# Causal attention on one Trainium2 core: the four diagonal squares of a block in one score tile, the rest of the diagonal unmasked

## The chip, the cores and the metric

The kernel runs on one core of a Trainium2 chip. The metric is device time in microseconds (us) of one execution: the median of the runs before is 1833.45 us.

The core has a matrix engine (TensorE, in the profile PE, with its weight loads as PEld), a vector engine (VectorE, DVE), a scalar engine (ScalarE, ACT), GpSimd (POOL) and an engine that issues DMAs (SyncE, SP). Each takes its own instructions in order; semaphores tie them together. TensorE writes its results into PSUM, which DVE and ACT read.

## What is computed

Two transformer layers on 2048 tokens of width 256. Each is a layer norm with causal attention (16 heads of 16), and a layer norm with an MLP (2048 wide, weights dequantised from packed codes). The first attention has rotary angles, biases and 4 key and value heads; the second has 16 and neither. What matters here is the attention:

```python
scores = jnp.einsum('bthd,bshd->bhts', q, k) * scale
causal = jnp.tril(jnp.ones((S, S), dtype=bool))
scores = jnp.where(causal[None, None, :, :], scores, -jnp.inf)
probs = jax.nn.softmax(scores, axis=-1)
attended = jnp.einsum('bhts,bshd->bthd', probs, v).reshape(B, S, hidden)
```

## The kernel before

**Units.** Queries go in 4 blocks `b` of 512 (4 tiles of 128), heads in 4 groups `g` of 4. A group is two pairs `p` of two heads `r`; the two heads of a pair lie in rows 0-63 and 64-127 of the matrix engine, so that two matmuls run side by side. A unit is one (b, g): 16 units per attention, 32 in all. Each unit has two passes over its keys.

**Maxima** (`max_steps`). For each block of keys `c` up to `b`, each query tile `i` and each pair, `scores` makes a score tile with queries on the partitions (L787), and DVE reduces it to a maximum per query and head (L799, tile `mx`). In the diagonal block, `c == b`, the tile is (i + 1) * 128 keys wide, and its last 128 columns, a square on the diagonal, are masked first. `gather` (L808) joins the maxima of the blocks and writes them as three bf16 parts into `m_pad`; `turn` (L826) transposes these on TensorE (L835), and ACT keeps them as `mT` (L841).

**Values** (`value_steps`). For each key tile `kt` and each pair, `pair` makes a score tile with keys on the partitions: first the "lift", which puts the negated maxima into PSUM (L884, weights `sel`), then the scores on top (L889). ACT takes the exponentials (L901) into `e`. On the diagonal, a tile begins at its own queries (`q0`), so that it is 512, 384, 256 or 128 columns wide, and its first 128 columns are masked. `values` multiplies `e` with the values and a column of ones, four heads in four column strips of the array (L869, f32, two instructions a matmul), into one accumulator `av`; it goes in halves of 256 queries. `end` copies `av` out, `divide` transposes it (L923) and divides.

**Masks.** `add_mask` (L756) adds very negative numbers to a 128x128 square by matmuls of a bf16 pair: two parts of 64 columns for each of two heads, so four matmuls of 64 columns (L762). They are not issued at once: the tile puts them, with what follows, into `self.owed`, and `settle` (L767) issues them at the next score tile of the kind, or at the next step of the value pass. Until then the tile stays in PSUM.

**PSUM.** A score tile is two banks, `[128, 2, 512]` f32, one per head. There are three of them, for both passes and the MLP (`ps_s`); `av` and a general tile `ps_m` have one bank each.

**Order.** It is written out by hand. `run` (L974) takes unit after unit: the value steps of this one are the main line, and beside them go the maxima of the next one, blended with preparations for the next block, output projections and dequantisation. `weave` (L43) spreads the side steps evenly over the main ones, with none beside the last three (`rest=3`). A main step is a tuple: its score tile, then the side steps, then its value matmuls. The first three steps of a unit have a share of their own (L1034 to L1036); the last unit's `end` and `divide` are put behind steps 0 and 2 of the next (L1025), and the next unit's `turn` ahead of the last step (L1028). The first unit's maxima run in the preparation of block 0, each followed by some idle matmuls (`fill`, L697). SP loads the queries of later units (`load_q`), GpSimd the keys (`load_k`).

Of the kernel before, what the change touches and what calls it, by code (L numbers as in the profile page):

```python
# [9 lines left out]
F32 = mybir.dt.float32  # L10
# [6 lines left out]
AF = mybir.ActivationFunctionType  # L17
# [4 lines left out]
P = 128  # L22
# [58 lines left out]
def tile_hybrid_layers(  # L81
# [329 lines left out]
    class Attention:  # L411
# [30 lines left out]
        def prep_steps(self, b, alone=False, load=False, picks=None, amid=(), fill=None):  # L442
# [245 lines left out]
            if picks:  # L688


                of = lambda f, c: lambda: f(c, krows if c == 2 else P)
                steps.append(lambda: fill(3))
                steps += [of(f, c) for c in (2, 0) for f in (pair, rotated_pair, high, low)]
                steps += [of(pair, 1), lambda: set_keys(2, krows), lambda: fill(2), set_queries]
                steps.append(lambda: fill(3))
                steps += [lambda: self.load_k(b, 2, 1), lambda: self.load_q(b, 1)]
                for step, idle in zip(amid, (0, 0, 1, 1, 2, 2, 2, 0, 1)):  # L697
                    steps += [step, lambda idle=idle: fill(idle)]
                steps[-1:-1] = [lambda: value(0), lambda: value(1)]
                self.after = [lambda: keep_value(0), lambda: keep_value(1)]  # L700
                self.after += [of(f, 1) for f in (rotated_pair, high, low)]
                self.after += [lambda: self.load_q(b, 2), add_bias]
                return steps
            else:
                kc = [*range(2, (D + krows + P - 1) // P)]
                for c in [*kc, 0, 1] if alone else [0, *kc, 1]:
                    n = min(P, D + krows - c * P)
                    if c == 1 and alone:
                        steps.append(values)
                    steps.append(holding(lambda c=c, n=n: plain(c, n)))  # L710
                    steps += [holding(lambda c=c, n=n: high(c, n)), lambda c=c, n=n: low(c, n)]
                    if c >= 2:
                        steps.append(lambda c=c: self.load_k(b, c))
                    elif c == 0 and load:
                        steps += [lambda g=g: self.load_q(b, g) for g in range(2)]
# [37 lines left out]
            return self.kT[c][64 * r : 64 * r + 64, g if self.first else 2 * g + p, at]  # L753

        @staticmethod
        def add_mask(pt, kind, at):  # L756

            for part in range(2):
                to = slice(at + 64 * part, at + 64 * part + 64)
                for r in range(2):  # L760
                    rows = slice(64 * r, 64 * r + 64)
                    nc.tensor.matmul(  # L762
                        pt[:, r, to], lhsT=mask_w[rows, kind, part, :],
                        rhs=mask_t[rows, kind, part, :], start=False, stop=(part == 1),
                    )

        def settle(self, kind=None):  # L767
# [8 lines left out]
        def max_steps(self, b, g):  # L776

            held = {}

            def scores(i, c, p):  # L780
                if not held:
                    held["mx"] = self.wk.tile([P, NT, 4, NB], F32, tag="mx", name="mx")
                w = TB if c < b else (i + 1) * P
                self.settle("max")
                pt = ps_s()
                for r in range(2):
                    nc.tensor.matmul(  # L787
                        pt[:, r, :w],
                        lhsT=self.qT[b, g][64 * r : 64 * r + 64, p, i * P : (i + 1) * P],
                        rhs=self.key_rows(c, g, p, r, slice(0, w)),  # L790
                        start=True, stop=(c < b),
                    )

                def masked():
                    self.add_mask(pt, 0, w - P)
                    reduced()

                def reduced():
                    nc.vector.tensor_reduce(  # L799
                        held["mx"][:, i, 2 * p : 2 * p + 2, c], pt[:, :, :w], AX.X, ALU.max  # L800
                    )

                if c == b:
                    self.owed.append(("max", masked))
                else:
                    reduced()

            def gather():  # L808
                self.settle()
                nm = self.wk.tile([P, NT, 4], F32, tag="nm", name="nm")  # L810
                nc.vector.tensor_reduce(
                    nm, held["mx"][:, :, :, : b + 1], AX.X, ALU.max, negate=True
                )

                to = m_pad[:, :, :, :6].rearrange("q t r (p s) -> q t p r s", s=3)
# [25 lines left out]
                nc.scalar.copy(self.mT[b, g], pt)  # L841


            tiles = [(i, c) for c in range(b + 1) for i in range(NT)]
            steps = [lambda i=i, c=c, p=p: scores(i, c, p) for i, c in tiles for p in range(2)]
            return steps + [gather], turn

        def value_steps(self, b, g):

            nk = NT * (b + 1)  # L850
            held = {"pending": []}

            def values(half):


                self.settle()
                kt, q0, es_ = held["pending"][0]
                whole = (b, g) == (NB - 1, NG - 1)
                few = whole or TB - q0 <= TB // 2
                if half == 1:  # L860
                    held["pending"].pop(0)
                if few and half != whole:
                    return
                if kt == 0 and half == whole:
                    held["av"] = ps_av()
                own = slice(q0, TB) if few else slice(*((q0, TB // 2), (TB // 2, TB))[half])
                for j in range(4):
                    h = g if self.first else 4 * g + j
                    nc.tensor.matmul(  # L869
                        held["av"][32 * j : 32 * j + 32, own],  # L870
                        lhsT=self.vv[kt // NT][:, kt % NT, h * VW : h * VW + 32],
                        rhs=es_[j // 2][:, j % 2, own],
                        start=(kt == 0 and half == whole), stop=(kt == nk - 1),
                    )

            def pair(kt, p):
                q0 = max(0, kt - NT * b) * P
                diagonal = kt >= NT * b
                keys = slice((kt % NT) * P, (kt % NT + 1) * P)
                self.settle()  # L880
                pt = ps_s()

                for r in range(2):
                    nc.tensor.matmul(  # L884
                        pt[:, r, q0:], lhsT=sel[64 * r : 64 * r + 64, p, :],
                        rhs=self.mT[b, g][64 * r : 64 * r + 64, q0:], start=True, stop=False,
                    )
                for r in range(2):
                    nc.tensor.matmul(  # L889
                        pt[:, r, q0:], lhsT=self.key_rows(kt // NT, g, p, r, keys),  # L890
                        rhs=self.qT[b, g][64 * r : 64 * r + 64, p, q0:],
                        start=False, stop=not diagonal,
                    )
                e = self.wk.tile([P, 2, TB], F32, tag="e", name="e", bufs=4)

                def masked():
                    self.add_mask(pt, 1, q0)
                    exponentials()

                def exponentials():  # L900
                    nc.scalar.activation(e[:, :, q0:], pt[:, :, q0:], AF.Exp, scale=QK_SCALE)  # L901

                if diagonal:
                    self.owed.append(("exp", masked))
                else:
                    exponentials()
                if p == 0:
                    held["es"] = [e]
                else:
                    held["pending"].append((kt, q0, held["es"] + [e]))  # L910

            def end():
                values(0)
                values(1)
                o = pre.tile([P, TB], F32, tag="o", name="o")
                nc.scalar.copy(o, held["av"])
                held["o"] = o
# [16 lines left out]
                )  # L934

            steps = []
            for kt in range(nk):
                for p in range(2):
                    scored = lambda kt=kt, p=p: pair(kt, p)
                    steps.append((scored, lambda p=p: values(p)) if kt else scored)  # L940
            return steps, end, divide

        def out_steps(self, b):
# [30 lines left out]
        def run(self, extra, beside):  # L974
# [17 lines left out]
            for n, (b, g) in enumerate(units):  # L992
# [30 lines left out]
                steps, end, divide = self.value_steps(b, g)  # L1023

                for at, step in zip((0, 2), ending):  # L1025
                    scored, *summed = steps[at] if isinstance(steps[at], tuple) else (steps[at],)
                    steps[at] = (scored, step, *summed)
                if turn:  # L1028
                    scored, summed = steps[-1]
# [1 line left out]
                if (b, g) == (0, 3):  # L1031

                    maxima = blend(maxima[:-1], [zeros] * 8) + maxima[-1:]
                first = len(maxima) * 3 // len(steps)  # L1034
                weave(steps[:3], lead + maxima[:first])
                weave(steps[3:], blend(maxima[first:], more) if maxima else more, rest=3)  # L1036
                ending = [end, divide]
            end()
            return [divide] + self.out_steps(NB - 1)
# [197 lines left out]
```

## Time and profile before

| | us |
|---|---|
| runs | 1833.45, 1830.45, 1834.42; median 1833.45 |
| span of the profiled execution | 1830.9 |
| median less that span | 2.55 |
| TensorE busy | 1748.1 |
| DVE busy | 1123.5 |
| ACT busy | 808.1 |
| first attention, first to last `mT` | 38.2 to 509.9 |
| second attention, first to last `mT` | 949.3 to 1454.0 |

The span is that of one profiled execution, and the profiler gives no other time for it; what the median has beyond the span lies around the first and last instruction. A busy TensorE is not TensorE at its peak, since matmuls are pipelined and a record's length has latency in it: distances between the starts of matmuls tell what they cost. A row of a group reads: line, engine, operation, output and inputs, count, busy time, mean ns of one, and the idle time of the engine before it with what ended it. Units of block 0 take 13 to 25 us from one `mT` to the next, those of block 3 some 46 to 52. The maxima of the first unit of an attention run ahead of it, so 32 units share one pattern; the last unit of each attention has no maxima beside it, but MLP work.

### The profile page before, as it was taken

To read this page: it belongs to the slowest core of one execution; us is meant where nothing else is said; L and a number is where in the kernel's file an instruction comes from. 1 tells how busy PE (TensorE), PEld (TensorE's weight loads), DVE (VectorE), ACT (ScalarE), POOL (GpSimd) and SP (SyncE) were. 2 spreads that over 40 slices of the span, in tenths; PEclk is the share of its full clock that TensorE was granted. 3 is DMA by queue.
4 is the path that set the end of the run, shared out by engine and by line. 5 is a ranking of instruction groups with operands and counts; after the bars stand their busy time and mean duration, and the time that the engine had idled before them with its cause. 6 is when DMAs were issued, how large, how long until landed. Compare 5 with 4: busy or idle time off the path is not lost.

```text
span 1830.9 us, 31568 instructions
## 1 busy us (share of the span) xinstructions
PE 1748.1 (95%) x13313; PEld 913.3 (50%) x13313; DVE 1123.5 (61%) x1679; ACT 808.1 (44%) x1080; POOL 239.8 (13%) x444
## 2 busy tenths in 40 slices
PE   8888899899999999999998999999999999999999
PEld 4444444444443474746464444444444445655646
DVE  5576887887884626262644767767877626354442
ACT  2435556566667313131314455655666753132221
POOL 4122202110013101012101000000000001111010
PEclk9899999999999999999999999999999999999999
DMA  5240400120002100005006132032000000000000
GB/s 139 68 93 32 94 24 30 48 50 24 19 13 76 52 1 0 1 0 125 2 1 117 24 76 53 22 60 59 13 13 2 11 37 1 12 3 9 7 6 12
DMA packets 43134, 65.40 MB, mean 36 GB/s; under 512 B 14000, under 2 KB 21040, under 8 KB 42736
## 3 DMA queue, kind: packets, MB, share of 16 engines
q1 hardware_dynamic: 34352, 47.37, 9.0%
q0 software_dynamic: 7680, 15.48, 4.9%
q8 instruction: 105, 1.72, 0.4%
q10 hardware_dynamic: 960, 0.52, 0.1%
q14 instruction: 37, 0.30, 0.1%
HBM read 43.45 MB, written 17.83 MB: 33 GB/s over the span
## 4 chain that ended last, share of the span: by engine, by line
PE 74%; DVE 15%; ACT 7%; issue 2%; DMA 1%; POOL 0%; ACTq 0%; DVEq 0%; SPq 0%; POOLq 0%
PE ps_s L1086 24%; DVE mx L799 12%; PE ps_av L869 10%; PE ps_s L884 7%; PE ps_s L787 6%; PE ps_m L1111 6%; PE ps_av L1111 6%; ACT e L901 5%; PE ps_s L889 5%; PE ps_m L504 2%; PE ps_m L963 2%; PE ps_s L762 1%; ACT mT L841 1%; PE ps_s L504 1%; PE ps_m L923 1%
## 5 line engine op out<-in xcount | busy, mean ns | idle before, releaser
L799 DVE TENSOR_REDUCE mx<-ps_s 128x2 f32<-128x1024 f32 (+3 forms) x640 | 660.3, 1061 | 216.7 <-PE ps_s L762 109.0
L901 ACT ACTIVATE e<-ps_s 128x1024 f32<-128x1024 f32 (+3 forms) x640 | 568.8, 898 | 374.1 <-PE ps_s L889 219.5
L869 PE MATMUL ps_av<-e,v 128*32 128x256 f32 (+2 forms) x4384 | 350.7, 391 | 0.0
L889 PE MATMUL ps_s<-qT,kT 64*128 64x512 f32 (+3 forms) x1280 | 333.8, 519 | 0.0
L787 PE MATMUL ps_s<-kT,qT 64*128 64x512 f32 (+3 forms) x1280 | 266.5, 418 | 34.2 <-DVE mx L799 15.3
L884 PE MATMUL ps_s<-mT,sel 64*128 64x512 bf16 (+3 forms) x1280 | 229.9, 353 | 26.1 <-ACT mT L841 11.0
L1086 PE MATMUL ps_s<-xnT,wg 128*128 128x512 f32 x512 | 240.9, 593 | 0.0
L1086 PE MATMUL ps_s<-xnT,wu 128*128 128x512 f32 x512 | 240.6, 592 | 0.0
L884 PEld LDWEIGHTS <-sel 64*128 64x128 bf16 x1280 | 75.5, 93 | 252.4 <-issue 241.8
L787 PEld LDWEIGHTS ps_s<-kT,qT 64*128 64x128 f32 x1280 | 127.6, 185 | 142.8 <-ACT e L901 67.3
L1092 ACT ACTIVATE t<-ps_s 128x512 f32<-128x512 f32 x128 | 76.3, 596 | 243.9 <-PE ps_s L1086 243.7
L1095 ACT ACTIVATE t<-t 128x512 f32<-128x512 f32 x128 | 80.6, 629 | 199.0 <-DVE t L1094 199.0
L1094 DVE TENSOR_TENSOR t<-ps_s,t 128x512 f32<-128x512 f32 x128 | 88.2, 689 | 123.3 <-POOL t L1093 121.1
L1086 PEld LDWEIGHTS ps_s<-xnT,wu 128*128 128x128 f32 x512 | 97.3, 190 | 122.5 <-issue 122.5
L1093 POOL TENSOR_SCALAR t<-t 128x512 f32<-128x512 f32 x128 | 79.0, 618 | 534.4 <-ACT t L1092 530.8
L1086 PEld LDWEIGHTS ps_s<-xnT,wg 128*128 128x128 f32 x512 | 95.1, 190 | 104.2 <-issue 102.5
L1096 DVE SCALAR_TENSOR_TENSOR t<-t,ps_s 128x512 f32<-128x512 f32 x128 | 88.0, 687 | 89.0 <-ACT t L1095 89.0
L869 PEld LDWEIGHTS ps_av<-e,v 128*32 128x32 f32 x4384 | 87.3, 108 | 93.2 <-issue 78.9
L889 PEld LDWEIGHTS ps_s<-qT,kT 64*128 64x128 f32 x1280 | 128.4, 195 | 0.0
L1111 PE MATMUL ps_m<-wd,inter 128*128 128x256 f32 x512 | 114.5, 380 | 0.0
L1111 PE MATMUL ps_av<-wd,inter 128*128 128x256 f32 x512 | 114.5, 380 | 0.0
L1111 PEld LDWEIGHTS ps_av<-wd,inter 128*128 128x128 f32 x512 | 96.7, 190 | 17.1 <-issue 4.5
(147 smaller groups left out, 1192.8 us busy)
## 6 DMA issues: line engine op xcount, KB each, us to landing
qT<-h SPq DMA_DIRECT2D x248, 64.0 KB, 2.2
kT<-h POOLq DMA_DIRECT2D x88, 128.0 KB, 5.8
h<-high SPq DMA_DIRECT2D x24, 256.0 KB, 2.1
h<-low SPq DMA_DIRECT2D x24, 256.0 KB, 3.1
wd<-wd_kept SPq DMA_DIRECT2D x2, 2048.0 KB, 8.2
wd_kept<-dq_d SPq DMA_DIRECT2D x4, 512.0 KB, 2.7
out<-x SPq DMA_DIRECT2D x16, 128.0 KB, 1.7
x<-x SPq DMA_DIRECT2D x3, 512.0 KB, 7.5
```

The lines of the kernel that those rows point to most:

```text
L787: nc.tensor.matmul(pt[:, r, :w], lhsT=self.qT[b, g][64 * r : 64 * r + 64, p, i * P : (i + 1) * P], rhs=self.key_rows(c, g, p, r, slice(0, w)),
L799: nc.vector.tensor_reduce(held["mx"][:, i, 2 * p : 2 * p + 2, c], pt[:, :, :w], AX.X, ALU.max)
L869: nc.tensor.matmul(held["av"][32 * j : 32 * j + 32, own], lhsT=self.vv[kt // NT][:, kt % NT, h * VW : h * VW + 32], rhs=es_[j // 2][:, j % ...
L884: nc.tensor.matmul(pt[:, r, q0:], lhsT=sel[64 * r : 64 * r + 64, p, :], rhs=self.mT[b, g][64 * r : 64 * r + 64, q0:], start=True, stop=False,)
L889: nc.tensor.matmul(pt[:, r, q0:], lhsT=self.key_rows(kt // NT, g, p, r, keys), rhs=self.qT[b, g][64 * r : 64 * r + 64, p, q0:], start=Fals ...
L901: nc.scalar.activation(e[:, :, q0:], pt[:, :, q0:], AF.Exp, scale=QK_SCALE)
L1086: nc.tensor.matmul(pt[:, k, :], lhsT=w[:, c, fc * P : (fc + 1) * P], rhs=self.xnT[b][:, c, :], start=(c == 0), stop=(c == 1),)
L1093: nc.gpsimd.tensor_scalar(t, t, GELU_A, 1.0, ALU.mult, ALU.add)
L1094: nc.vector.tensor_tensor(t, gate, t, ALU.mult)
L1095: nc.scalar.activation(t, t, AF.Tanh, scale=GELU_C)
L1096: nc.vector.scalar_tensor_tensor(t, t, 1.0, gate, ALU.add, ALU.mult)
L1111: nc.tensor.matmul(po[:, :D], lhsT=inter[:, fc, i * P : (i + 1) * P], rhs=wd[:, fc, :], start=(fc == 0), stop=(fc == NFC - 1),)
```

## The change

In the diagonal block both passes are cut otherwise. The four 128x128 squares on the diagonal, one per query tile, go side by side into one score tile per pair; one set of four mask matmuls, now 256 columns each (64 in each of the four squares), masks them all. What is left under the diagonal needs no mask:

- Maxima: query tile 3 has 384 keys per pair, in a tile as before. Query tiles 2 and 1 have 256 and 128 keys per pair; both pairs go side by side into one tile. The unmasked part's maxima have a column of their own in `mx` (`NB + 1` columns); query tile 0 has no such part, and GpSimd writes the very negative number there. Six tiles in place of eight, in the order 3, 3, squares, squares, 2, 1.
- Values: key tile 0 of the block has 384 queries per pair, key tiles 1 and 2 have 256 and 128, both pairs in one tile. Six tiles in place of eight, in the order 0, 0, squares, squares, 1, 2. The value matmuls are `rest(0)`, 384 wide, behind the first squares; `own`, 4 x 4 of 128 columns, behind key tile 1; `rest(1)` behind key tile 2; `rest(2)` in `end`.
- Score matmuls: 28 in place of 16 per unit and pass, with the same columns in all. Mask matmuls: 16 in place of 64 per unit. Value matmuls on the diagonal: 28 in place of 24.
- `run`: in block 0 one step, not three, has its own share. In the first preparation, seven maximum steps with five idle matmuls take the place of nine with nine.

```diff
-                for step, idle in zip(amid, (0, 0, 1, 1, 2, 2, 2, 0, 1)):
+                for step, idle in zip(amid, (0, 0, 1, 1, 2, 0, 1)):
...
+                    to = pt[:, r, :].rearrange("p (n c) -> p n c", c=P)
                     nc.tensor.matmul(
-                        pt[:, r, to], lhsT=mask_w[rows, kind, part, :],
-                        rhs=mask_t[rows, kind, part, :], start=False, stop=(part == 1),
+                        to[:, :, 64 * part : 64 * part + 64], lhsT=mask_w[rows, kind, part, :],
+                        rhs=mask_t[rows, kind, part, :].unsqueeze(1).broadcast_to([64, NT, 64]),
+                        start=False, stop=(part == 1),
                     )
...
+                    held["mx"] = self.wk.tile([P, NT, 4, NB + 1], F32, tag="mx", name="mx")
+                    nc.gpsimd.memset(held["mx"][:, 0, :, b + 1], NEG)
                 self.settle("max")
                 pt = ps_s()
...
+                if c < b:
+                    product(pt, 0, i, c, p, slice(0, TB))
+                    maximum(mx[:, i, heads, c], pt)
+                elif i == 0:
+                    for n in range(NT):
+                        at = n * P
+                        product(pt, at, n, b, p, slice(at, at + P), n == 0, False)
+
+                    def masked():
+                        self.add_mask(pt, 0)
+                        maximum(
+                            mx[:, :, heads, b], pt.rearrange("q r (n k) -> q n r k", k=P)
+                        )
+
                     self.owed.append(("max", masked))
+                elif i == NT - 1:
+                    product(pt, 0, i, b, p, slice(0, i * P))
+                    maximum(mx[:, i, heads, b + 1], pt[:, :, : i * P])
                 else:
+                    for n in range(2):
+                        product(pt, n * i * P, i, b, n, slice(0, i * P))
+                    maximum(
+                        mx[:, i, :, b + 1].rearrange("q (p r) -> q p r", r=2),
+                        pt[:, :, : 2 * i * P].rearrange("q r (p k) -> q p r k", p=2),
+                    )
...
+            tiles = [(i, c, p) for c in range(b) for i in range(NT) for p in range(2)]
+            tiles += [(i, b, p) for i in (NT - 1, 0) for p in range(2)]
+            tiles += [(i, b, 0) for i in (2, 1)]
...
+            def both_pairs(kt):
+                q0 = (kt + 1 - first) * P
+                queries, w = slice(q0, TB), TB - q0
+                self.settle()
+                pt = ps_s()
+                for p in range(2):
+                    lift(pt, p * w, p, queries, p == 0)
+                for p in range(2):
+                    score(pt, p * w, p, kt, queries, p == 1)
+                e = held["e"][kt] = new_e()
+                exponentials(e[:, :, : 2 * w], pt[:, :, : 2 * w])
+
+            def squares(p):
+                self.settle()
+                pt = ps_s()
+                lift(pt, 0, p, slice(0, TB))
+                for n in range(NT):
+                    score(pt, n * P, p, first + n, slice(n * P, (n + 1) * P), False)
+                e = held["e"]["own", p] = new_e()
+
+                def masked():
+                    self.add_mask(pt, 1)
+                    exponentials(e, pt)
+
+                self.owed.append(("exp", masked))
...
+            def own():
+                self.settle()
+                for n in range(NT):
+                    to = slice(n * P, (n + 1) * P)
+                    product(
+                        first + n, to, lambda j: held["e"]["own", j // 2][:, j % 2, to]
+                    )
...
             steps = []
-            for kt in range(nk):
+            for kt in range(first + 1):
                 for p in range(2):
...
+            steps += [
+                (lambda: squares(0), lambda: rest(0)), (lambda: squares(1),),
+                (lambda: both_pairs(first + 1), own),
+                (lambda: both_pairs(first + 2), lambda: rest(1)),
+            ]
...
+                some = 3 if b else 1
+                first = len(maxima) * some // len(steps)
+                weave(steps[:some], lead + maxima[:first])
+                weave(steps[some:], blend(maxima[first:], more) if maxima else more, rest=3)
```

`first` is the first key tile of the unit's own block, `product` in the value pass makes four matmuls, one per head.

## The prediction

> **What bounds the kernel now.** I first read the share of each engine, the chain that ended last and the costliest groups, all on the page:
>
> ```profile
> PE 1748.1 (95%) x13313; PEld 913.3 (50%) x13313; DVE 1123.5 (61%) x1679; ACT 808.1 (44%) x1080; POOL 239.8 (13%) x444
> ...
> PE 74%; DVE 15%; ACT 7%; issue 2%; DMA 1%; POOL 0%; ACTq 0%; DVEq 0%; SPq 0%; POOLq 0%
> ...
> L884 PE MATMUL ps_s<-mT,sel 64*128 64x512 bf16 (+3 forms) x1280 | 229.9, 353 | 26.1 <-ACT mT L841 11.0
> ```
>
> TensorE ends 74% of the span. What DVE adds (15%) comes in pairs of reductions during which TensorE waits for a score tile. The third line shows one wait for `mT` in each of the 32 units, 0.34 us (11.0 / 32). Then the groups by shape:
>
> ```profile
> L799 DVE TENSOR_REDUCE mx<-ps_s 128x2 f32<-128x1024 f32 x448 | 533.1, 1221 | 122.2 <-PE ps_s L787 99.2 <-PE ps_s L762 15.3
> ...
> L762 PE MATMUL ps_s<-mask_t,mask_w 64*128 64x64 bf16 x2048 | 100.9, 195 | 0.0
> ...
> L799 DVE TENSOR_REDUCE mx<-ps_s 128x2 f32<-128x256 f32 x64 | 26.6, 421 | 34.8 <-PE ps_s L762 34.0
> ...
> L835 PE MATMUL ps_m<-ident_b,m_pad 128*128 128x128 bf16 x128 | 12.7, 222 | 4.9 <-DVE m_pad L822 4.5
> ```
>
> 2048 mask matmuls are 64 per unit, in 16 groups of four. A reduction costs about 154 ns plus 1.042 ns an element: (1221 − 421) / 768 and the remainder. TensorE's durations contain pipeline latency, so its costs are taken as distance between starts. The end of a unit on TensorE, one row per group:
>
> ```profile
> 1357.87 0.28 PE L884 MATMUL ps_s<-mT,sel 64*128 64x256 bf16 x2
> 1357.91 0.36 PE L889 MATMUL ps_s<-qT,kT 64*128 64x256 f32 x2
> 1358.12 0.23 PE L762 MATMUL ps_s<-mask_t,mask_w 64*128 64x64 bf16 x4
> 1358.28 0.43 PE L869 MATMUL ps_av<-e,v 128*32 128x128 f32 x8
> 1358.64 0.28 PE L884 MATMUL ps_s<-mT,sel 64*128 64x256 bf16 x2
> ...
> 1359.04 0.64 PE L869 MATMUL ps_av<-e,v 128*32 128x256 f32 x8
> 1359.62 0.23 PE L884 MATMUL ps_s<-mT,sel 64*128 64x128 bf16 x2
> 1359.65 0.31 PE L889 MATMUL ps_s<-qT,kT 64*128 64x128 f32 x2
> 1359.80 0.23 PE L762 MATMUL ps_s<-mask_t,mask_w 64*128 64x64 bf16 x4
> ...
> 1361.61 0.39 PE L884 MATMUL ps_s<-mT,sel 64*128 64x512 bf16 x2 [0.32 <-ACT mT L841]
> ```
>
> Lift and scores of a tile take 0.25 us at 256 columns, 0.18 at 128 (elsewhere 0.35 at 384, 0.46 at 512). Eight value matmuls take 0.36 at 128 columns and 0.57 at 256, so 0.785 at 384. Until the last line nothing waits: the diagonal end of a unit is TensorE's. One more row gives the price of a fresh set of weights under a short matmul:
>
> ```profile
> 34.34 2.00 PE L640 MATMUL ps_av<-wqkv_a,xnT 128*128 128x64 f32 x16
> 36.17 0.38 PE L1146 MATMUL ps_m<-zeros 128*128 128x512 bf16 x1
> ```
>
> 16 matmuls, each with its own 128 columns of f32 weights, come 114 ns apart (1.83 / 16), although they move only 64 columns.
>
> **The change, part by part, per unit** (32 units). Columns stream at 0.417 ns (a 512-wide pair of score matmuls, rows 0-63 and 64-127 at once, follows the last after 213).
>
> 1. Masks. Four 64-wide ones take 67 ns when scores follow, of which 2 x 27 stream. 16 groups: 1,072. After: 4 groups of 2 x 107 + 13 = 227, together 908. **−0.16.** The columns stay the same, only the overhead goes. A matmul that writes four pieces of 64 with gaps is nowhere in the trace; bounds 908 and 4 x 4 x 67 = 1,072, and I take 908 since streaming is what both rows share. The Trainium skill, PSUM — Partial Sum Buffer, section Specifications (TRN2), speaks against it: an access pattern that is not contiguous "slows matmuls significantly". No row here tests it; at half rate, my estimate, the masks would cost 1.7 and the kernel 27 us more.
>
> 2. Squares. A 512-wide score pair becomes four 128-wide pairs, each with weights of its own; nothing stands between them, so the next pair's load lies under 53 ns of streaming only. I take 115 a pair, the row above: three pairs of four are 62 longer, four such tiles: **+0.74.** Bounds: 53 a pair (load hidden, +0) and 146 (the transposes at L923, four in 0.585 us, also a load each; +1.12). The Trainium skill, TensorE: Matmul & The Clock Gate, section Back-to-back issue gap, gives about 81 ns for a 128-column matmul in a stream of load and matmul; by it the squares would cost 0.34 and the sum would be 13 us lower. The 114 measured here is for f32 weights, and I keep it.
>
> 3. Both pairs in one tile. Maxima: second load under 107 or 53 of streaming, +0.01 and +0.06. Exponentials: 0.474 for two of 0.244, 0.366 for two of 0.186, −0.02. **+0.05.**
>
> 4. Values. Before: groups of 0.57, 0.57, 0.36, 0.57, 0.57, 0.36: 3.00. After: 0.785, eight sets of four at 133 plus 92 to leave (from the 0.36 and 0.57) = 1.156, 0.57, 0.36: 2.87. Two groups fewer; entering one costs 90 (score pair to value matmul 508, to score pair 418). **−0.31.**
>
> 5. Tiles. Two maximum tiles fewer; about half of them wait for a tile to come free and then show a load of some 105. **−0.11.** DVE and ACT have two instructions fewer each, 0.31 and 0.34 (ACT by 1027 and 386: about 172 an instruction). Off the path while TensorE ends the unit.
>
> TensorE: −0.16 + 0.74 + 0.05 − 0.31 − 0.11 = **+0.21**, times 32 = +6.8 us.
>
> 6. A new wait. The value matmuls of the squares (`own`) follow the first two-pair tile, and need the exponentials of the second square tile. Those start 0.12 after its mask and take 1.03, landing 0.05 later; TensorE has 0.47 of scores and 0.09 of entering to do: **+0.63**, times 32 = +20.2. Queued behind it on TensorE: the rest of `own`, `turn`, the last tile. No maxima are left to fill it: `weave` with rest=3 puts none beside the last three steps.
>
> 7. Waits that go. `rest(1)` (0.66 with entry) now stands between `turn` and the next unit, and hides `mT`: 30 x 0.34 = −10.2. `gather` is issued some 4 us before `turn` instead of 2.3, so the wait for `m_pad` goes: −4.5.
>
> 8. Tile turnover. In the diagonal phases TensorE waits 17.5 us for a reduction or exponential (added up from its idle rows: 10.8 in the units of block 0, 4.6, 1.9 and 0.2 in blocks 1 to 3). 12 tiles instead of 16 turn over, 4 instead of 16 are held for a mask. Bounds 0 and −17.5; I take half: −8.8.
>
> 9. Pace before the diagonal. Maxima go into two steps fewer: block 3 has 28 in 24 instead of 30 in 26, block 2 has 20 in 16 instead of 22 in 18, block 1 has 12 in 8 instead of 14 in 10. At 1.22 a reduction DVE needs 1.5 to 7% more per dense step, about 0.3 a unit, 21 units: 0 if TensorE paces them, +6.5 if DVE does; half: +3.2.
>
> 10. GpSimd gets a memset per unit for the extra column of `mx` (0.15 to 0.17, rows L437 and L439); only `gather`, a unit later, needs it. Behind GpSimd's longest issue (eight `kT` loads, 4 us) it is still in time: 0. In block 0 one step instead of three leads a unit, with two slots for the rest as before: 0. Prologue: four idle matmuls and two reductions less, −0.5. No DMA moves in the program's order past another. The squares' reduction writes eight rows instead of two; bounds 1,221 and four starts more (1,221 + 4 x 154). I take 1,221: the small reduction at L811 writes 16 rows from 64 elements in 0.22 us.
>
> Sum: 6.8 + 20.2 − 10.2 − 4.5 − 8.8 + 3.2 − 0.5 = **+6.2 us**. The profiled span is 1830.9; around it lie some 2.6 to the median of 1833.45. So 1837.1 as span, **1840** as time.
>
> **Rivals.**
> - *Faster: turnover was the price.* If all 17.5 us of item 8 go, and `own` waits little because its first matmuls and the loads cover it (half, −10): 6.2 − 8.7 − 10 = −12.5, **1821**. If the squares' loads hide completely, −24 alone: **1816**. It decides where TensorE's rows show 53 to 80 ns between the square's pairs. For it: block 0 waits most and is all diagonal. Against: blocks 2 and 3 hardly wait there.
> - *No change:* the gains of items 7 and 8 and the wait of item 6 cancel within a few us, **1834**.
> - *Slower by DVE's idle end.* After `gather` TensorE has about 5 us alone before the next reduction, where the trace has 2.65 to 2.85 in block 3. If DVE is what paces the stretch before (its reductions fill 0.74 to 0.87 of most units), its 2 to 3 us more of idling are paid in a third of the units: 10 x 1.2, plus the full 6.5 of item 9: **1855**. With 146 a pair it would be 1867.
> - *The clock.* From 44 to 58 us the granted clock is 0.51, from 75 to 79 it is 0.59. If the shorter prologue moves this stretch in or out, ±7.
> - *The change doing nothing* is excluded: 64 masks against 16.
>
> **How the numbers follow.** Forecast (1836 to 1846) 0.36; slower by DVE 0.20; faster 0.30; no change 0.14. This measurement can tell 0.2%, 3.7 us: within 1829.8 to 1837.1 counts as same. The forecast reaches slightly into it, and the faster case too: faster 0.30, same 0.16, slower 0.54. The range takes in hidden loads below and DVE's end above: 1815 to 1860; signs being mixed, the likeliest case alone is 1836 to 1846.
>
> **What would show it.** Right: square pairs 110 to 120 ns apart, an idle of about 0.6 us before `own` ended by ACT `e`, no wait for `mT` or `m_pad`, mask groups of about 0.23. Wrong: pairs at 60 to 80, no idle before `own`, a reduction of the squares well above 1.22, mask groups above 0.27, or a longer dense phase with TensorE waiting for DVE `mx`.

## The result, and the profile after

The changed kernel takes **1845.99 us**, the median of four runs from 1843.23 to 1851.67; the kernel before takes 1832.32 beside it (four runs, 1830.45 to 1834.42). The ratio is 1.008, with a 95% interval from 1.0061 to 1.01: slower by 13.7 us, where 6.2 had been worked out. The profiled execution after took 1843.23, its span is 1841.4.

The page after: share of the engines, and the groups of the lift and of the value matmuls.

```profile
PE 1747.1 (95%) x12814; PEld 941.9 (51%) x12829; DVE 1111.1 (60%) x1615; ACT 797.4 (43%) x1016; POOL 242.1 (13%) x476
...
L939 PE MATMUL ps_av<-e,v 128*32 128x256 f32 (+3 forms) x4672 | 352.1, 378 | 11.3 <-ACT e L894 11.2
...
L877 PE MATMUL ps_s<-mT,sel 64*128 64x512 bf16 (+3 forms) x1280 | 219.8, 355 | 13.8 <-DVE mx L789 5.5
```

TensorE has 499 matmul records fewer, yet is busy for only one us less. The wait for `mT` before the lift is nearly gone, 1.3 us in all (a reduction's `mx` is now what the lift waits for most), and the value matmuls have a wait that they did not have: 11.2 us, ended by the exponentials. The groups by shape:

```profile
L789 DVE TENSOR_REDUCE mx<-ps_s 128x8 f32<-128x1024 f32 x64 | 77.3, 1220 | 33.4 <-PE ps_s L761 33.0
...
L761 PE MATMUL ps_s<-mask_t,mask_w 64*128 64x256 bf16 x512 | 53.1, 289 | 0.3 <-issue 0.3
```

The reduction of the four squares writes eight rows and takes 1220 ns. The masks are 512 instructions in place of 2048. The end of a unit on TensorE, the stretch that corresponds to the timeline shown of before:

```profile
1367.69 0.85 PE L939 MATMUL ps_av<-e,v 128*32 128x384 f32 x8
1368.47 0.39 PE L877 MATMUL ps_s<-mT,sel 64*128 64x512 bf16 x2
1368.51 0.75 PE L886 MATMUL ps_s<-qT,kT 64*128 64x128 f32 x8
1369.10 0.39 PE L761 MATMUL ps_s<-mask_t,mask_w 64*128 64x256 bf16 x4
1369.33 0.38 PE L877 MATMUL ps_s<-mT,sel 64*128 64x256 bf16 x4
...
1369.87 0.41 PE L939 MATMUL ps_av<-e,v 128*32 128x128 f32 x4
1370.67 1.07 PE L939 MATMUL ps_av<-e,v 128*32 128x128 f32 x28 [0.38 <-ACT e L894]
1371.67 0.40 PE L851 MATMUL ps_m<-ident_b,m_pad 128*128 128x128 bf16 x4
...
1372.44 0.64 PE L939 MATMUL ps_av<-e,v 128*32 128x256 f32 x8
1373.01 0.39 PE L877 MATMUL ps_s<-mT,sel 64*128 64x512 bf16 x2
```

The 384-wide value matmuls take 0.78 (1367.69 to 1368.47), a mask group 0.23, the lift and scores of the squares 0.63 up to the masks. `own` begins at 1369.87 with the heads of the first pair, those of the second pair wait for their exponentials, and it ends with `turn` at 1371.67: 1.80 in all, against 1.156 without a wait. By starts the wait is thus 0.64; the row of waits counts less of it, 0.36 a time (11.2 / 31), since the records of the first heads run on into it. The waits of TensorE, as us in total, times, and the longest:

```profile
PE ps_s L782 <- DVE mx L789: 29.8, 56, 1.4
PE ps_av L939 <- ACT e L894: 11.2, 31, 0.4
PE ps_s L782 <- ACT e L894: 7.6, 21, 0.4
PE ps_s L877 <- DVE mx L789: 5.5, 13, 0.6
...
PE ps_s L877 <- ACT mT L857: 1.3, 2, 0.7
```

and of before:

```profile
PE ps_s L787 <- DVE mx L799: 15.3, 34, 1.3
PE ps_s L787 <- ACT e L901: 15.0, 36, 1.3
PE ps_s L884 <- ACT mT L841: 11.0, 32, 0.7
PE ps_s L884 <- DVE mx L799: 4.7, 14, 0.5
PE ps_m L835 <- DVE m_pad L822: 4.5, 10, 0.9
```

The waits for `mT` and `m_pad` are all but gone, as worked out. The tile waits (the rows of `ps_s` ended by `mx` or `e`) were 39.2 us before, 4.2 that the lift waited for `e` included, and are 45.2 after, with 2.3 of that kind. They did not fall.

**Where the time went.** Time from one `mT` to the next adds up to stages (the first attention's sixteenth and last `mT` of before comes at 556.6; 509.9 is its fifteenth); the differences between the two profiles, in us:

| stage | after less before | half-rate time before, after |
|---|---|---|
| prologue | −1.2 | 0, 0 |
| block 0, both attentions | −1.7, **+10.7** | 17.1, 20.5 and 0, 23.9 |
| block 1 | +1.0, +2.5 | 0, 3.4 and 0, 0 |
| blocks 2 and 3 | −1.0, −0.3, −0.7, −2.4 | 0, 0 |
| last units with MLP, and tail | +2.4, +1.3 | 0, 0 |

The third column is time at half the clock. Windows of both kernels in block 0 of the second attention show it (columns: window, length, busy us and instructions of PE, PEld, DVE, ACT, POOL, then the granted clock, the busy share of the DMA engines and GB/s). After:

```profile
955.00:962.00 7.00, 5.92 (x56) 3.43 (x56) 4.69 (x12) 2.37 (x3) 1.10 (x2) 0.52 0.00 0
962.00:975.00 13.00, 10.86 (x121) 6.55 (x112) 5.39 (x7) 5.46 (x9) 0.00 (x0) 1.00 0.20 62
975.00:986.00 11.00, 8.84 (x42) 4.15 (x44) 4.10 (x11) 1.61 (x2) 2.55 (x5) 0.53 0.32 98
```

and before:

```profile
955.00:962.00 7.00, 5.84 (x78) 2.73 (x78) 6.66 (x17) 1.61 (x4) 1.04 (x1) 1.00 0.00 0
962.00:975.00 13.00, 11.30 (x126) 6.26 (x126) 5.25 (x12) 6.58 (x10) 0.00 (x0) 1.00 0.15 45
975.00:986.00 11.00, 9.07 (x116) 4.75 (x114) 5.79 (x12) 4.36 (x9) 3.94 (x8) 1.00 0.50 133
```

PE is about equally busy in all of them: a busy PE does not say at what clock. Over the span the mean granted clock fell from 0.995 to 0.987, so half-rate time (twice one less the clock, times the span) rose from some 17 to some 48 us. What one us of it costs can be read from repeated runs of one and the same kernel, since it varies by itself: 21 runs of the kernel before go from 1830.43 us with 14.6 at half rate to 1836.27 with 33.0, a slope of 0.28; the four runs after go from 1843.23 with 47.9 to 1851.67 with 70.3, a slope of 0.38. By a third, my estimate from these two, the extra 33 us of the median runs (55 against 22) are worth some 11 of the 13.7. This is rough: the slopes of the kernels under Experiments go from 0.13 to 0.33, and with 0.13 it would be 4.

The Trainium skill, TensorE: Matmul & The Clock Gate, section What's actually happening, tells of two clocks, 1.2 and 2.4 GHz, chosen after windows of about 3.4 us by how busy the array was. The half-rate stretches of after are 3.4, 6.8 and 10.2 us long, and before has one of 13.7, all multiples of 3.41, in keeping with it. What the page calls an idle window is not to be read as a TensorE without work, though. The clock falls at 954.91 and at 975.39; in the 3.41 us ahead of each, still at the full clock, the records of TensorE fill 59% and 53%:

```profile
951.50:954.91 3.41, 2.01 (x34) 1.79 (x32) 3.34 (x8) 0.00 (x0) 0.00 (x0) 1.00 0.02 5
971.98:975.39 3.41, 1.80 (x28) 1.41 (x24) 3.31 (x3) 0.36 (x1) 0.00 (x0) 1.00 0.20 77
```

Before has 87% in the first of these windows (2.98 of 3.41) and keeps its clock. The share alone does not decide it: after has 54% from 64.03 to 67.44 (1.85 of 3.41), and the clock stays full behind it.

### The profile page after: what moved, and what is told of

Its sections match the earlier page's. It is cut to its first block, busy times and chain, and to the rows that moved or that the text cites. A ratio compares the mean times of both kernels' runs of the same rounds, so it can differ in the third digit from the quotient of the medians.

```text
span 1841.4 us, 30444 instructions
## 1 busy us (share of the span) xinstructions
PE 1747.1 (95%) x12814; PEld 941.9 (51%) x12829; DVE 1111.1 (60%) x1615; ACT 797.4 (43%) x1016; POOL 242.1 (13%) x476
## 4 chain that ended last, share of the span: by engine, by line
PE 57%; DVE 8%; ACT 3%; issue 1%; POOL 0%; ACTq 0%; POOLq 0%
PE ps_s L1152 24%; DVE mx L789 6%; PE ps_av L939 6%; PE ps_m L1177 6%; PE ps_av L1177 6%; PE ps_s L877 3%; PE ps_s L782 3%; PE ps_s L886 3%; ACT e L894 2%; PE ps_m L504 1%; PE ps_m L1028 1%; PE ps_s L761 1%; PE ps_m L640 1%; PE ps_m L979 0%; PE ps_m L1128 0%
## 5 line engine op out<-in xcount | busy, mean ns | idle before, releaser
L789 DVE TENSOR_REDUCE mx<-ps_s 128x2 f32<-128x1024 f32 (+3 forms) x576 | 648.7, 1161 | 238.5 <-PE ps_s L782 198.4
L894 ACT ACTIVATE e<-ps_s 128x1024 f32<-128x1024 f32 (+1 forms) x576 | 555.2, 978 | 391.8 <-PE ps_s L886 282.5
L939 PE MATMUL ps_av<-e,v 128*32 128x256 f32 (+3 forms) x4672 | 352.1, 378 | 11.3 <-ACT e L894 11.2
L877 PE MATMUL ps_s<-mT,sel 64*128 64x512 bf16 (+3 forms) x1280 | 219.8, 355 | 13.8 <-DVE mx L789 5.5
L782 PEld LDWEIGHTS ps_s<-kT,qT 64*128 64x128 f32 x1664 | 145.2, 191 | 148.1 <-DVE mx L789 76.7
L877 PEld LDWEIGHTS <-sel 64*128 64x128 bf16 x1280 | 67.4, 93 | 227.9 <-issue 217.8
L939 PEld LDWEIGHTS ps_av<-e,v 128*32 128x32 f32 x4672 | 102.3, 108 | 132.6 <-issue 100.8
L886 PEld LDWEIGHTS ps_s<-qT,kT 64*128 64x128 f32 x1664 | 151.3, 196 | 2.4
```

Of the source, the lines that this page charges most:

```text
L782: nc.tensor.matmul(pt[:, r, at : at + keys.stop - keys.start], lhsT=self.qT[b, g][64 * r : 64 * r + 64, p, i * P : (i + 1) * P], rhs=self. ...
L789: nc.vector.tensor_reduce(to, pt, AX.X, ALU.max)
L877: nc.tensor.matmul(pt[:, r, at : at + queries.stop - queries.start], lhsT=sel[64 * r : 64 * r + 64, p, :], rhs=self.mT[b, g][64 * r : 64 * ...
L886: nc.tensor.matmul(pt[:, r, at : at + queries.stop - queries.start], lhsT=self.key_rows(kt // NT, g, p, r, keys), rhs=self.qT[b, g][64 * r ...
L894: nc.scalar.activation(e, pt, AF.Exp, scale=QK_SCALE)
L939: nc.tensor.matmul(held["av"][32 * j : 32 * j + 32, to], lhsT=self.vv[kt // NT][:, kt % NT, h * VW : h * VW + 32], rhs=of(j), start=openin ...
```

## Experiments

Two theories stood at the start. The **wait theory**: the new wait before `own` is the loss, and the rest of the change gains what was worked out. The **clock theory**: the wait is mostly harmless, and the idle times that the new cut brings to block 0 lower the granted clock. Ratios are to the kernel before on the same chip, 1833.55 us (21 runs) for the first four, 1833.45 (11 runs) for the others.

**e1_warm.** After, with an idle matmul of 512 columns ahead of the tiles of block 0, 52 in all (11 us by 213 ns each).

```diff
# scores (maxima), after pt = ps_s()
+                if b == 0 and g:
+                    warm(pt)
# squares (values)
+                if b == 0:
+                    warm(pt)
# warm(pt)
+        nc.tensor.matmul(pt[:, 0, :], lhsT=sel[:, 0, :], rhs=nothing, start=True, stop=True)
```

> The changed kernel plus one idle matmul of 512 columns (bf16, 0.21 us at full clock) into each new maximum tile of block 0 (not the first unit) and each value square tile of block 0: 52 in all, 11 us of streaming. Two theories. Clock theory: the 14 us that the change costs are mostly the clock gate; block 0's wide tiles leave windows in which TensorE streams too little, and half-rate time went from 17 us to 48 us. Then half-rate time falls below 25 us and the time to 1832 to 1840, although work is added. Wait theory: every unit pays some 0.4 us for the squares' weight loads and the wait before the squares' value matmuls, the clock is a side effect. Then the fillers can only add: 1846 to 1857.

1843.55 us (1842.34 to 1843.89), ratio 1.0051, 1.0038 to 1.0063. Its profile has a span of 1841.8 and a clock of 0.995. The idle matmuls give the clock back (17.1 us at half rate in place of 47.8), and the time falls by only 2.4. Both expectations missed. In block 0 of the second attention half-rate time fell from 23.9 to 6.8, and the stage stayed at 88.1 against 88.0: half the idle matmuls, 5.5 us, stand there. If they cost all of that, the 17.1 us of better clock gave as much, which makes 0.32 us per us, near the slope of the repeated runs; if some of them stood where TensorE waited anyway, the clock's price is lower. That it has a price is seen directly under e5. Idle matmuls are no free way to save it.

**e2_old0.** After, with block 0 of both attentions cut as before.

```diff
+            if not (b > 0):
+                return self.max_steps_old(b, g)
...
+            if not (b > 0):
+                return self.value_steps_old(b, g)
```

> The changed kernel with both passes of block 0 cut as before (and the prologue and the first share as before), blocks 1 to 3 as changed. Clock theory: half-rate time back at about 17 us, time 1827 to 1834, at or below the kernel before. Wait theory: the 24 units of blocks 1 to 3 still pay 0.4 us each, 1840 to 1844.

1837.88 us (11 runs, 1835.46 to 1843.99), ratio 1.0029, 1.0018 to 1.004. Both expectations missed: the time lies between them, and the median run, with a clock of 0.992, has some 29 us at half rate. Block 0 of the second attention is 78.1, nearly as before (77.3). The new cut of block 0 is thus worth some +8 of the 13.7 (1845.99 − 1837.88). In the profile, which is of a slower run (1840.96), that stage is 9.9 shorter than in after, but block 1 of the first attention is 3.9 longer, with 13.7 us at half rate in place of 3.4.

**e3_own_late.** After, with the value matmuls of the squares one step later, where their exponentials are long done.

```diff
-                (lambda: both_pairs(first + 1), own),
-                (lambda: both_pairs(first + 2), lambda: rest(1)),
+                (lambda: both_pairs(first + 1),),
+                (lambda: both_pairs(first + 2), lambda: (own(), rest(1))),
```

> The changed kernel with the squares' value matmuls one step later, behind the last two-pair tile, so that they no longer wait for the exponentials (31 waits, 11.2 us of TensorE in the changed kernel). Wait theory: nearly all of it comes back, 1834 to 1837. Clock theory: the waits outside block 0 come back in part (24 x 0.36 = 8.6 at most, 4 to 8 expected), half-rate time stays above 30 us, time 1838 to 1842.

**1816.95 us** (1814.61 to 1817.41), ratio 0.9905, 0.9892 to 0.9919: 29 us below after, and faster than both kernels, more than either theory had said. The end of a unit now reads

```profile
1347.88 1.57 PE L939 MATMUL ps_av<-e,v 128*32 128x128 f32 x40
1349.39 0.39 PE L877 MATMUL ps_s<-mT,sel 64*128 64x512 bf16 x2
```

`own` and `rest(1)` together take 1.51 (1347.88 to 1349.39). After needs 1.80 and 0.57 (`rest(1)`, 1372.44 to 1373.01): 0.86 more, and unit by unit blocks 2 and 3 are shorter by 0.85 (46.86 to 46.00, 51.05 to 50.21). Of it 0.64 is the wait (1.80 less 1.156), and 0.22 the merging of two groups (1.156 + 0.57 − 1.51). 32 times 0.86 is 27.5. Blocks 2 and 3 run at the full clock in both kernels, so their 0.85 is not the clock's. Over the whole profile half-rate time is 41.0 in place of 47.8, worth some 2 of the 26.2 between the spans by a third.

**e4_no_idle.** The kernel before, without 72 of its idle matmuls (15 us by 213 ns).

```diff
-                for _ in range(4 if (b, g) <= (1, 0) else 0):
+                for _ in range(0):
...
-                    maxima = blend(maxima[:-1], [zeros] * 8) + maxima[-1:]
+                    maxima = maxima[:]
```

> The kernel before without its 72 idle matmuls of block 0 (8 x 2 per attention between the maxima ahead of block 1, 4 ahead of each of the first turns): 15 us less of TensorE work. Clock theory: half-rate time rises well above 17 us, to 35 or more, and the time does not fall, 1832 to 1850. Wait theory, in which the clock has no great price: 1820 to 1830.

1832.44 us (11 runs, 1829.51 to 1837.54), ratio 0.9995, 0.9986 to 1.0004: no difference, as the clock theory expected. The clock falls to 0.986, and 51.2 us at half rate in place of 17.1 stand against 15 us of work saved. As in e1, the two cancel. By a third the 34 us would cost only 11, so by that estimate some of the idle matmuls had stood where TensorE waited anyway.

**e5_idle_in_wait.** After, with three idle matmuls (0.64 us) between the first two-pair tile and `own`, 96 in all.

```diff
-                (lambda: both_pairs(first + 1), own),
+                (lambda: both_pairs(first + 1), lambda: (idle(), own())),
# idle: three times
+                    nc.tensor.matmul(pt, lhsT=sel[:, 0, :], rhs=nothing, start=True, stop=True)
```

> The changed kernel plus three idle matmuls of 512 columns (0.64 us at full clock) in every unit between the first two-pair tile and the squares' value matmuls, where TensorE waits for the exponentials: 96 in all, 20 us of streaming put into the wait itself. If the wait is the 0.63 us of the prediction, the fillers cost nothing and blocks 1 to 3 stay within 0.2 us a unit. What is left tells the price of the clock apart. Clock theory (half-rate time explains most of block 0's loss in the second attention, 88.0 against 77.3 us): half-rate time falls below 25 us and the time to 1834 to 1840. Queue theory (block 0 loses because three wide reductions stand on DVE ahead of the preparation's subtraction, which TensorE waits for): half-rate time may fall, the time stays at 1843 to 1849.

1850.24 us (1847.8 to 1851.74), ratio 1.0096, 1.0083 to 1.0109. Blocks 2 and 3 stay as after to 0.1 us (165.2, 145.6, 163.2, 142.1): 0.64 us of work fits into the wait, which confirms its size there. But the half-rate time did not fall below 25 as expected. The profile, of the slowest of the four runs, has some 61 us, and over the four runs the clock is 0.983 to 0.986, no better than after's 0.981 to 0.987. Why these matmuls did not hold the clock is open.

The prologue gives the clock's price apart. It has the same instructions as in after, since the edit stands behind it, and up to the first maxima the two are 0.16 us apart. Then the clock of this execution is at half from 31.11 to 41.35. From the first score matmul of the maxima to the first lift, e5 and then after (columns as above):

```profile
27.93:41.58 13.65, 12.21 (x65) 7.62 (x66) 8.26 (x16) 0.58 (x1) 3.19 (x12) 0.62 0.37 83
27.77:37.69 9.92, 7.85 (x65) 5.18 (x67) 8.03 (x16) 0.59 (x1) 3.13 (x11) 1.00 0.60 118
```

The same 65 matmuls take 3.73 us longer with 10.24 us at half rate: 0.36 per us, without any change of work. It also shows that one and the same piece of program gets half rate in one execution and not in another.

**e6_maxima_only** and **e7_values_only.** One pass cut anew, the other as before (`value_steps`, or `max_steps`, of the kernel before).

```diff
# e6: value_steps of the kernel before; in run
-                some = 3 if b else 1
+                some = 3
# e7: max_steps of the kernel before, and its idle matmuls in the first preparation
```

> Only the maxima are cut in the new way, the values as before (so no squares' wait, and three steps lead a unit in every block). Theory of the wait: without the value pass the loss outside block 0 is gone; the new maxima have 0.37 of weight loads and save 0.08 of masks and two tiles of turnover: 1828 to 1836. Rival: the maxima's wide reductions in block 0 are the loss: 1838 to 1846, and the second attention's block 0 at 84 us or more.

1824.38 us (1823.44 to 1827.99), ratio 0.9961, 0.9949 to 0.9973: −9.1, better than expected.

> Only the values are cut in the new way, the maxima as before (one step leads a unit in block 0). Theory of the wait: the 0.85 us a unit are all here, and so are the waits for mT and m_pad that go: blocks 2 and 3 within 1 us a block of the changed kernel, time 1835 to 1845, block 0 of the second attention near 80 us. Rival (the maxima's reductions are not to blame for block 0): block 0 of the second attention at 86 us or more.

1853.11 us (1852.65 to 1854.33), ratio 1.0114, 1.01 to 1.0129: +19.7, worse than expected. The two add up to +10.6, about the +12.5 of the whole (1845.99 − 1833.45). Tile waits (as above) are 27.7 us in e6 and 48.9 in e7, against 39.2 before: the maxima's cut alone frees the tiles, the values' cut alone holds them longer. The two differences, −11.5 and +9.7, do not add up to the +6.0 of the whole. In e7 blocks 2 and 3 lose only 3.3 us in sum, though block 2 is some 3 us longer than in after, where 1 was expected; the rest is in block 0 (+6.1 in each attention, with 51.2 us at half rate in place of 17.1) and the last units (+3.5 and +1.3, where e6 has −0.8 and 0.0). So what after loses in the last units (+2.4, +1.3) comes with the values' cut.

**e8_late_old20.** e3, with block 0 of the second attention alone cut as before.

```diff
# e3's edit, and in max_steps and value_steps
+            if not (b > 0 or self.first):
+                return self.max_steps_old(b, g)        # value_steps_old
```

> The squares' value matmuls one step later, and block 0 of the second attention alone cut as before. Both theories of block 0 expect its 4 to 5 us back on top of the late value matmuls (1817): 1811 to 1815. If block 0 of the second attention stays at 81 us or more, its loss comes from what stands around it.

1814.41 us (6 runs, 1811.52 to 1821.79), ratio 0.9909, 0.9892 to 0.9925. The time is as expected, and that stage is 78.1 as in e2, 3.8 less than e3's 81.9. The median is the lowest of all, but its interval overlaps e3's almost wholly, so that a gain over e3 is not shown.

## Why the prediction came out near, point by point

The time is 1846 where 1840 was forecast, slower as forecast. The prices of the new tiles and the new wait were right, but that the sum came out near is luck: two errors of opposite sign nearly cancel. By the terms in the table below, blocks 2 and 3 would have lost some 7 us (14 units by 0.5); they gained 4.4. Everything else would then have come out about even (6.2 less 7); it lost 15 (the 10.5 between the spans, and 4.4).

- **Items 1 to 4, the new tiles: right as single prices.** Mask group 0.229 (227 worked out), squares of the maxima 397 ns up to their masks (398), 384-wide values 785 (785), `own` without a wait and with it 1.80 (1.79). The square pairs are 109 to 117 ns apart from the second on, as in the row of the prologue and not the 81 of the Trainium skill (TensorE: Matmul & The Clock Gate, Back-to-back issue gap). The masks that write four pieces of 64 cost what their columns stream, 229 ns; the slowing that the Trainium skill tells of (PSUM — Partial Sum Buffer, Specifications (TRN2)) does not show here.
- **The same items, what they remove: too small.** Blocks 2 and 3 run at the full clock in both profiles, so their TensorE rows can be added up by distance between starts (14 units, us per unit; waits and 0.09 for each entry into value matmuls taken out of the rows):

| | before | after | difference | the prediction's terms |
|---|---|---|---|---|
| masks | 1.34 | 0.94 | −0.41 | −0.16 |
| scores and lifts, both passes | 20.49 | 20.76 | +0.26 | +0.68 |
| values, entries, and the wait of `own` | 17.18 | 17.27 | +0.09 | +0.32 |
| waits for `mT`, `m_pad`, tiles | 1.46 | 1.13 | −0.33 | −0.3 |

  With 0.04 of other rows these units gain 0.35 each, where the terms had made them lose 0.5. A mask group before cost 0.084 (1.34 / 16), not the 0.067 read from the few rows ahead of a score tile; and the tiles that go were worth more than item 5's 0.11. How the 0.42 by which the second row is off splits between tiles and loads was not tried; the squares' loads cost what was worked out (the 398 above).
- **Item 6, the wait of `own`: right.** 0.64 against 0.63, shown by e3 and e5; 32 times it is 20.5 us. That `rest(1)` could be merged with it for another 0.22 was not seen.
- **Item 7: right.** Waits for `mT` went from 11.0 to 1.3, for `m_pad` from 4.5 to none.
- **Items 8 and 9, turnover and pace: wrong sign.** Together −5.6 was taken; the tile waits rose by 6.0 (39.2 to 45.2). Block 1 shows it at its plainest: waits for `mx` there went from 4.3 to 8.6 and from 3.6 to 7.0, and it is longer by 3.5. Fewer steps alone do not explain these: e7 has the same steps, and 4.8 and 3.9 there. e6 and e7 show why half the turnover was no good middle: the maxima's cut alone does give turnover (−11.5), and the values' cut alone, with two steps fewer for the reductions to spread over, costs 9.7. Why the two together come to +6.0 is open.
- **Item 10: right.** The memset takes 105 ns; 0.2 us in all wait for it. The prologue gave 1.2 where 0.5 was taken. That the single leading step of block 0 costs nothing was not tried by itself.
- **The clock: the missing term.** It stood among the rivals with ±7 for two stretches in block 0 of the first attention, and at nothing in the sum. That stage changed little (17.1 to 20.5 us at half rate); block 0 of the second attention went from none to 23.9. With the 27.3 more of both block 0 stages, a third each makes +9, which is what the two stages lost (−1.7 + 10.7). The agreement is in part luck: stage by stage a third makes +1.1 and +8.0, and the wait of `own` (4 by 0.64 in each) and the gains elsewhere are in the stages too.

That block 0 loses its clock there is shown by the windows and by e2 and e8. What begins it is read from one profile only. At each of the two falls TensorE waits for DVE. Ahead of the first it waits 1.40 us for a score tile that a reduction holds. At the second, three of the wide reductions, one after another, hold DVE, and the subtraction that the preparation of the next block needs stands behind them:

```profile
954.63 0.58 PE L782 MATMUL ps_s<-kT,qT 64*128 64x256 f32 x4 [1.40 <-DVE mx L789]
...
972.08 3.49 DVE L789 TENSOR_REDUCE mx<-ps_s 128x8 f32<-128x1024 f32 x3 [3.63 <-PE ps_s L761]
...
975.49 0.68 DVE L581 TENSOR_TENSOR low<-ps_m,high 128x512 fp32r<-128x512 f32 x1
...
976.22 3.78 PE L504 MATMUL ps_m<-xnT,wqkv_b 128*128 128x512 f32 x4 [2.36 <-DVE low L581]
```

TensorE idles 2.36 us for it, the clock falls within this time, and the four matmuls behind it then take 3.78 where the same four took 1.98 at 969.73. But e3 has the same waits with less time at half rate (13.7). How much of the stage is DVE's queue and how much the clock it leads to is not settled beyond the price in e1 and e5.

Of the rivals, "slower by DVE's idle end" had the right engine and place (waits for `mx`) but its gap in block 3 cost nothing: block 3 gained. Of "turnover was the price", e6 shows a part for the maxima alone: tile waits fell by 11.5 and the time came to 1824. That e3 came to 1817, near that rival's 1816, is not its mechanism: the squares' loads do not hide (109 to 117 ns a pair), and e3's tile waits are 45, as after's.

## What to carry over

When work is merged into fewer and larger tiles, look at who consumes the last one: value matmuls placed one step too early cost 0.64 us a unit, some 20 us in all, and hid a gain of 1%, and the cure was to move one call. Price what a change removes by the rows of all its neighbours, not by the cheapest position, and try the two halves of a change apart, since here one gained 9 us and the other lost 20. In a stage with slack on TensorE, work out the granted clock too: fewer instructions there may only trade streaming for half-rate time.

## What the runs showed of the hardware

- Half-rate time cost 0.13 to 0.38 us for each us, by the slope over repeated runs (e1 0.13, e3 0.16, e4 0.21, e5 0.25, before and e6 0.28, e2 and e8 0.33, after 0.38; the four runs of e7 have one clock). The clock is given to three digits, so the slopes of few runs are rough. Where the same 65 matmuls ran at both clocks (prologue of e5 and after), it was 0.36. It goes with most of the spread between runs of one kernel (correlation 0.96 in 21 runs of before).
- The clock fell behind windows of 3.41 us in which TensorE's records filled 59% and 53%, so a TensorE with work can lose it; behind one with 54% it stayed.
- Taking 72 idle matmuls out of the kernel before changed nothing (0.9995, 0.9986 to 1.0004): 15 us of work against 34 us more at half rate (51.2 in place of 17.1).
- Mask matmuls that write four pieces of 64 columns, 128 columns from one start to the next, cost 229 ns for four of 256 columns, two of them side by side; two streams of 107 are 214. A reduction of 1024 elements that writes eight values in place of two takes 1220 ns against 1221.
